# A feed-forward beside a recurrence: the gelus as one block on ACT, and fewer recurrence units planned around them

## Chip, core and metric

The kernel runs on one core of a Trainium2 chip, in one launch, in float32. The metric is the device time of one execution in microseconds. A core has five engines that matter here, each with its own in-order queue: PE (TensorE, matrix products and transposes), DVE (VectorE), ACT (ScalarE), POOL (GpSimd) and SP (SyncE, which issues most DMAs).

## What is computed

The input is 8 images of 384 channels and 32 x 32 pixels, so 8 sequences of 1024 tokens. Two layers follow each other. Cut to what matters here:

```python
# layer 0: RMS norm, then a selective recurrence in both directions
deltaA, deltaBu = exp(delta * A), (delta * u) * Bm
h[t] = deltaA[t] * h[t-1] + deltaBu[t]        # 16 states of 384 channels
y[t] = sum_n h[t, n] * Cm[t, n]
x = x + res_scale * ((fwd + bwd) * scale_mod + sigmoid(dwconv(xn)) * xn)
# layer 1
t = t + causal_attention(layernorm(t))         # 6 heads
# feed-forward, all of it per sequence; only the first 5 of 8 sequences are non-zero
y = layernorm(t) @ Wb1.T + b1                  # 384 -> 1536, weights binarized by group
hq = clip(y * 128 / (max(abs(y)) + 1e-5), -128 + 1e-5, 128 - 1e-5)
y2 = gelu(hq) @ Wb2.T + b2                     # 1536 -> 384
t = t + clip(y2 * 128 / (max(abs(y2)) + 1e-5), -128 + 1e-5, 128 - 1e-5)
```

The quantization divides by the maximum over the whole sequence. So no gelu may start before the last element of the first product is known, and no element of the output before the last of the second.

## The kernel before

The eight sequences are worked on in the order 0, 1, 2, 3, 5, 6, 4, 7. Each goes through three kinds of work: `before_scan` (norm, input projection L341, convolutions by taps L369 and L400, gates L434 and L453, the delta steps L518 to L531), the recurrence, and `attention` with `feed_forward` behind it for sequences 0 to 4.

**The recurrence** is cut into 768 units, 96 a sequence. A unit is two of the 16 states, one block of 128 channels and half of the tokens in one direction. `s_first` multiplies on POOL (L588) into one of six buffers g; `s_scan` makes two exponentials on ACT into two PSUM banks `da` (L601), two scans on DVE (L606), sometimes a copy of the carry on POOL (L611), and the second multiplication on POOL (L612); `s_sum` adds up eight 128 x 128 transposes on PE (L620), after which the g buffer is free. A slot of the plan issues the first multiplication of unit k + 2, the scan and second multiplication of unit k and the transposes of unit k - 1. POOL's order is pinned, so it is L588 of k + 2, then L612 of k. The loads of `bc`, `ud` and `dl` go through SP (line 112), as do those of the weights w1 and w2.

**The feed-forward** of a sequence is, in program order: layernorm; twelve blocks of 128 features in two halves, each three matmuls (L993), a bias-add on ACT (L1001), and per block a maximum on DVE (L1003); `quant_scale`, which reduces the maxima to one, spreads it with one transpose on PE (L960) and makes 128 / (max + 1e-5) in four small DVE operations (L962 to L965); four gelus on ACT of 128 x 3072 elements (L1018), each followed by the load of the table set that exponentials and logarithms use (L1019) and a clip on DVE (L1020); then for three blocks of 128 channels in two halves twelve matmuls each (L1038), a bias-add on ACT and a maximum on DVE; `quant_scale` again; and the output.

**The order of the work.** All of this is recorded as a list of steps with planned costs in us (`emit.of(...)`). The feed-forwards of sequences 0 to 3 are interleaved with the `before_scan` of sequences 5, 6, 4 and 7, by the share of the planned cost that each has used up (`spread_over`); the costs of both then count 0.6 (`JOINT`). The feed-forward of sequence 4 stands alone. The slots of the recurrence are spread evenly over the planned time of attention and feed-forward between due dates. So a step's planned cost decides how many slots, and how many steps of the other sequence, are issued around it; it costs nothing itself. A scheduler then moves instructions within priorities: `tc.high_priority(offset=60)` lifts a step's instructions ahead of others, `pin` (`tc.keep_in_program_order`) holds the order on their engine.

Of the kernel before, what the change touches and what calls it, by code (L numbers as in the profile page):

```python
# [11 lines left out]
AF = mybir.ActivationFunctionType  # L12
ALU = mybir.AluOpType
# [7 lines left out]
NC = C // P  # L21
# [9 lines left out]
NF = FF // P  # L31
GROUPS = 5
QMAX = 128.0
QEPS = 1e-5
QCLIP = QMAX - QEPS
# [11 lines left out]
LOG_EXP = "natural_log_exp_and_others"  # L47
# [7 lines left out]
def kernel(  # L55
# [16 lines left out]
    nc = tc.nc  # L72
    pin = tc.keep_in_program_order
# [13 lines left out]
    def btile(name):  # L87
        return big.tile([P, NC, L], F32, name=name, tag="big")

    def mtile(name, n=L):  # L90
        return mid.tile([P, n], F32, name=name, tag="mid")
# [7 lines left out]
    def bank(name, tag=None):  # L99
        if tag is None:  # L100
            turn[0] += 1
            tag = ("s", "pt")[turn[0] % 2]
        return ps.tile([P, HB], F32, name=name, tag=tag, bufs=BANKS[tag])

    def half(h):
        return slice(h * HB, (h + 1) * HB)

    def chunk(c):
        return slice(c * P, (c + 1) * P)

    def load(dst, src):
        nc.sync.dma_start(out=dst, in_=src)
# [167 lines left out]
    def layernorm(src, name, emit):  # L280

        dst = src
        st = {}
        for h in range(NH):

            @emit.of(6.0)
            def _(h=h):
                mean = mean_of(lambda c: src()[:, c, half(h)], f"mean_{name}_{h}")
                for c in range(NC):
                    nc.vector.tensor_tensor(  # L290
                        dst()[:, c, half(h)], src()[:, c, half(h)], mean, ALU.subtract
                    )
                st[h] = squares(dst(), h, name)

        for h in range(NH):

            @emit.of(6.0)
            def _(h=h):
                var = mean_of(lambda c: st[h][c], f"var_{name}_{h}")
                rstd_of(var, 1)  # L300
                for c in range(NC):
                    nc.vector.tensor_tensor(  # L302
                        dst()[:, c, half(h)], dst()[:, c, half(h)], var, ALU.mult
                    )
# [369 lines left out]
    def attention(b, emit_ffn, emit):  # L674
# [276 lines left out]
        if feeds:  # L951
            feed_forward(b, lambda: st["t2"], emit_ffn)


    def quant_scale(mx, name):

        col = small.tile([P, 1], F32, name=f"col_{name}", tag="col")
        nc.vector.tensor_reduce(col, mx, AX.X, ALU.max)
        row = bank(f"row_{name}", "s")
        nc.tensor.transpose(row[:, :P], col.to_broadcast([P, P]), ident)  # L960
        s = small.tile([P, 1], F32, name=f"qs_{name}", tag="qs")
        nc.vector.tensor_reduce(s, row[:, :P], AX.X, ALU.max)  # L962
        nc.vector.tensor_scalar(s, s, QEPS, None, ALU.add)
        nc.vector.reciprocal(s, s)
        nc.vector.tensor_scalar(s, s, QMAX, None, ALU.mult)  # L965
        return s

    def feed_forward(b, t, emit):
        st = {}

        @emit
        def _():
            st["xn"] = t()
            st["mxh"] = small.tile([P, NF], F32, name=f"mxh_{b}", tag="mxh", bufs=1)
            st["mxy"] = small.tile([P, NC], F32, name=f"mxy_{b}", tag="mxy", bufs=1)

        layernorm(t, f"nf_{b}", emit)
        for m in range(NF):
            for h in range(NH):

                @emit.of(3.1)
                def _(m=m, h=h):
                    if m % NC == 0 and h == 0:
                        st["h", m // NC] = btile(f"h{m // NC}_{b}")
                    if m % 2 == 0 and h == 0:
                        st["w1"] = mtile(f"w1_{b}_{m}").rearrange("p (c e) -> p c e", c=4)
                        load(
                            st["w1"][:, :NC, :],
                            w1s[:, m * P : (m + 2) * P].rearrange("(c p) e -> p c e", p=P),
                        )  # L990
                    hp = bank(f"hp_{b}_{m}_{h}", "s")
                    for c in range(NC):
                        nc.tensor.matmul(  # L993
                            out=hp,
                            lhsT=st["w1"][:, c, chunk(m % 2)],
                            rhs=st["xn"][:, c, half(h)],
                            start=(c == 0),
                            stop=(c == NC - 1),
                        )
                    hm = st["h", m // NC][:, m % NC, :]  # L1000
                    nc.scalar.activation(hm[:, half(h)], hp, AF.Identity, bias=b1t[:, m : m + 1])  # L1001
                    if h == NH - 1:
                        nc.vector.tensor_reduce(  # L1003
                            st["mxh"][:, m : m + 1], hm, AX.X, ALU.max, apply_absolute_value=True
                        )

        @emit.of(12.0)
        def _():
            st["s1"] = quant_scale(st["mxh"], f"h_{b}")


        for q in range(NF // NC):

            @emit.of(4.0)
            def _(q=q):
                hq = st["h", q]
                with tc.high_priority(offset=60):
                    nc.scalar.activation(hq, hq, AF.Gelu, scale=st["s1"])  # L1018
                    tc.keep_in_program_order(nc.scalar.preload_act_table_set(LOG_EXP))  # L1019
                nc.vector.tensor_scalar(hq, hq, QCLIP, None, ALU.min)  # L1020

        for m in range(NC):
            for h in range(NH):

                @emit.of(10.7)
                def _(m=m, h=h):
                    if m == 0 and h == 0:
                        st["y"] = btile(f"yf_{b}")
                    if h == 0:
                        for k in range(0, NF, 6):  # L1030
                            w = mtile(f"w2_{b}_{m}_{k}", 6 * P).rearrange("p (k e) -> p k e", k=6)
                            load(
                                w, w2s[k * P : (k + 6) * P, chunk(m)].rearrange("(k p) e -> p k e", p=P)
                            )
                            st["w2", k // 6] = w
                    yp = bank(f"yp_{b}_{m}_{h}", "s")
                    for k in range(NF):
                        nc.tensor.matmul(  # L1038
                            out=yp,
                            lhsT=st["w2", k // 6][:, k % 6, :],  # L1040
                            rhs=st["h", k // NC][:, k % NC, half(h)],
                            start=(k == 0),
                            stop=(k == NF - 1),
                        )
                    ym = st["y"][:, m, :]
                    nc.scalar.activation(
                        ym[:, half(h)], yp, AF.Identity, bias=vec[:, m, V_B2 : V_B2 + 1]
                    )
                    if h == NH - 1:
                        nc.vector.tensor_reduce(  # L1050
                            st["mxy"][:, m : m + 1], ym, AX.X, ALU.max, apply_absolute_value=True
                        )

        @emit.of(12.0)
        def _():
            st["s2"] = quant_scale(st["mxy"], f"y_{b}")

        for m in range(NC):

            @emit  # L1060
            def _(m=m):
                to = mtile(f"t3_{b}_{m}")
                load(to, spilled[b, "t2", m])
                for h in range(NH):
                    ym = bank(f"yq_{b}_{m}_{h}", "s")
                    nc.vector.tensor_scalar(
                        ym, st["y"][:, m, half(h)], st["s2"], QCLIP, ALU.mult, ALU.min
                    )
                    th = to[:, half(h)]
                    nc.vector.scalar_tensor_tensor(th, ym, -QCLIP, th, ALU.max, ALU.add)  # L1070
                nc.sync.dma_start(out=out[b, chunk(m), :], in_=to)
# [151 lines left out]
```

## Time and profile before

| | |
|---|---|
| median of 6 runs | 5051.09 us (5039.68 to 5060.6) |
| profiled execution, its own time | 5039.68 us |
| its span | 5037.9 us |
| granted PE clock, mean | 0.883 |
| gelus, L1018, 20 of 128 x 3072 | 2.856 us each |
| table loads at L1018 and at L1019 | 19 and 19, 1.283 us each |
| clips, L1020 | 1.753 to 3.874 us, median 1.761 |
| memory traffic | 138 GB/s over the span |

The profile is that of the fastest of the six runs; its span and its own time differ by 1.8 us. It begins with some 127 us in which POOL has no unit yet, and ends with some 205 us of the last attention, in which the recurrence is over. Between them lie four rounds of attention with a joint feed-forward (829 to 3543 us), two rounds of attention alone (3543 to 4270) and one of attention with the lone feed-forward (4270 to 4829).

How to read it: busy us of an engine are the union of its instructions. In a row of a group the number before the vertical bar is what the group works on, then follow its busy us and the mean ns of one, and behind the second bar the idle time of the engine just before its instructions, with what ended most of it. A matmul in float32 leaves two records. L620 records are one transpose each, eight a unit.

### The profile page before, as it was taken

What the parts mean: (1) busy time and instruction counts of PE and PEld (TensorE: products, weight loads), DVE (VectorE), ACT (ScalarE), POOL (GpSimd) and SP (SyncE); (2) the same over time, 40 slices, a digit from 0 to 9 for tenths busy, and PEclk for the clock granted to TensorE, in tenths of its full rate; (3) what the DMA queues carried; (4) which work ended last, traced back from release to release, by engine and by line L of the source; (5) the groups of instructions that cost most, each with busy time, mean ns of one, the idle gap of its engine ahead of it and who ended that gap; (6) DMA issues with size and microseconds to landing.
All of it is one profiled execution on the core that took longest, in us unless ns stands there. A gap on an engine that the chain in (4) does not pass through costs nothing. (4 is left out here: it accounts for less than half of the span.)

```text
span 5037.9 us, 50760 instructions
## 1 busy us (share of the span) xinstructions
PE 4092.0 (81%) x16458; PEld 2188.9 (43%) x16458; DVE 3599.8 (71%) x4780; ACT 2719.8 (54%) x4891; POOL 3691.0 (73%) x1944
## 2 busy tenths in 40 slices
PE   3687787878788888888797888888788978878899
PEld 1243343544434444444443445434444544444444
DVE  6887978677786778876678867678767666666523
ACT  4565664565645656545556446565365454464426
POOL 0578687987669986788876698768788978787710
PEclk7788797989889898888998899998998989989999
DMA  6554546324363334443334533335533324324210
GB/s 232 198 176 157 207 155 229 113 86 142 132 217 116 118 114 162 161 172 124 103 134 142 204 108 130 113 117 188 181 129 122 101 96 143 105 93 134 87 64 26
DMA packets 365010, 696.36 MB, mean 138 GB/s; under 512 B 30104, under 2 KB 88904, under 8 KB 364744
## 3 DMA queue, kind: packets, MB, share of 16 engines
q1 hardware_dynamic: 355232, 676.97, 39.6%
q10 hardware_dynamic: 9512, 16.15, 0.9%
q8 instruction: 130, 2.13, 0.2%
q14 instruction: 136, 1.11, 0.1%
HBM read 527.33 MB, written 165.68 MB: 138 GB/s over the span
## 5 line engine op out<-in xcount | busy, mean ns | idle before, releaser
L588 POOL TENSOR_TENSOR g<-ud,bc 128x1024 f32<-128x1024 f32 x768 | 1837.9, 2393 | 644.8 <-PE y L620 506.6
L612 POOL TENSOR_TENSOR g<-g,bc 128x1024 f32<-128x1024 f32 x768 | 1820.4, 2370 | 229.9 <-DVE g L606 177.3
L601 ACT ACTIVATE da<-dl,amat 128x512 f32<-128x512 f32 x1536 | 1056.4, 691 | 1486.6 <-DVE g L606 1443.9
L606 DVE TENSOR_TENSOR_SCAN g<-da,carry,g 128x512 f32<-128x512 f32 x768 | 958.3, 1272 | 408.4 <-POOL g L588 366.2
L606 DVE TENSOR_TENSOR_SCAN g<-da,g 128x512 f32<-128x512 f32 x768 | 906.8, 1211 | 472.7 <-POOL g L588 440.3
L620 PE MATMUL y<-ident,g 128*128 128x128 f32 x6144 | 935.0, 300 | 273.8 <-POOL g L612 214.2
L620 PEld LDWEIGHTS y<-ident,g 128*128 128x128 f32 x6144 | 774.1, 154 | 731.1 <-POOL g L612 340.5
L786 PE MATMUL s<-k,q 64*128 64x512 f32 (+3 forms) x1152 | 404.7, 609 | 126.0 <-DVE nm L800 114.9
L800 DVE CUSTOM_DVE_ANT_0 pr<-s,cmask 128x512 f32<-128x512 f32 (+3 forms) x576 | 301.0, 546 | 207.6 <-PE s L786 181.7
L810 ACT ACTIVATE pr<-pr,nm 128x512 f32<-128x512 f32 (+3 forms) x576 | 348.9, 607 | 139.6 <-DVE nm L800 137.8
L862 PE MATMUL pt<-ident,pr 128*128 128x128 f32 x1728 | 301.8, 305 | 72.3 <-ACT ptn L864 32.9
L993 PE MATMUL hp<-t,w 128*128 128x512 f32 x720 | 337.2, 613 | 26.7 <-DMA w<-w1s 13.8
L1038 PE MATMUL yp<-h,w 128*128 128x512 f32 x720 | 328.2, 613 | 9.8 <-DMA w<-w2s 9.8
L341 PE MATMUL in<-xn,win 128*128 128x512 f32 x576 | 296.1, 656 | 46.0 <-DVE xc L463 14.8
L862 PEld LDWEIGHTS pt<-ident,pr 128*128 128x128 f32 x1728 | 208.7, 153 | 234.0 <-ACT ptn L864 87.9
L875 PE MATMUL av<-ptn,v 128*64 128x512 f32 (+3 forms) x1152 | 273.3, 557 | 24.0 <-DVE o L889 16.2
L864 ACT COPY ptn<-pt 128x512 f32<-128x512 f32 (+3 forms) x576 | 255.1, 474 | 67.6 <-PE pt L862 66.2
L400 DVE SCALAR_TENSOR_TENSOR loc<-xn,vec,loc 128x496 f32<-128x496 f32 (+3 forms) x384 | 260.7, 723 | 23.6 <-ACT loc L389 22.2
L725 PE MATMUL qp<-t,wqk 128*128 128x512 f32 x576 | 261.2, 603 | 19.0 <-DVE t L302 13.5
L611 POOL COPY carry<-g 128x2 f32<-128x2 f32 x384 | 85.6, 223 | 242.8 <-DVE g L606 242.8
L786 PEld LDWEIGHTS s<-k,q 64*128 64x128 f32 x1152 | 139.2, 208 | 254.4 <-DVE nm L800 192.5
L1038 PEld LDWEIGHTS yp<-h,w 128*128 128x128 f32 x720 | 140.1, 199 | 177.3 <-issue 166.2
(155 smaller groups left out, 4803.0 us busy)
## 6 DMA issues: line engine op xcount, KB each, us to landing
bc<-rows SPq DMA_DIRECT2D x512, 512.0 KB, 4.0
dl<-sdl SPq DMA_DIRECT2D x160, 256.0 KB, 2.9
ud<-sud SPq DMA_DIRECT2D x160, 256.0 KB, 2.7
t<-st SPq DMA_DIRECT2D x63, 512.0 KB, 5.0
su<-u SPq DMA_DIRECT2D x48, 512.0 KB, 3.9
du<-su SPq DMA_DIRECT2D x96, 256.0 KB, 4.7
sdl<-du SPq DMA_DIRECT2D x96, 256.0 KB, 3.2
sud<-du SPq DMA_DIRECT2D x96, 256.0 KB, 2.5
```

What stands on the lines that cost most here:

```text
L341: nc.tensor.matmul(out=mp, lhsT=st["win", c][:, k, i, :], rhs=st["xn"][:, k, half(h)], start=(k == 0), stop=(k == NC - 1),)
L588: pin(nc.gpsimd.tensor_tensor(g, ud, sst["bc", 0, u.b, u.part, u.n], ALU.mult))
L601: nc.scalar.activation(da, sst["dl", u.b, u.c, u.part], AF.Exp, scale=amat[:, u.c, n : n + 1])
L606: nc.vector.tensor_tensor_scan(gi[:, ::step], da[:, ::step], gi[:, ::step], first, ALU.mult, ALU.add)
L612: pin(nc.gpsimd.tensor_tensor(g, g, sst["bc", 1, u.b, u.part, u.n], ALU.mult))
L620: nc.tensor.matmul(out=y[:, j, :], lhsT=g[:, i, chunk(j)], rhs=ident, is_transpose=True, start=(u.opens and i == 0 and j == 0), stop=(u.cl ...
L786: mm = nc.tensor.matmul(out=ss[e][:, : k1 - k0], lhsT=st["q"][rows_of(e), c, chunk(qi)], rhs=st["k"][rows_of(e), c, k0:k1], start=True, st ...
L800: nc.vector.tensor_tensor_reduce(out=x, in0=ss[e][:, :w], in1=mask, scale=-1.0, scalar=-MASKED, op0=ALU.add, op1=ALU.min, accum_out=m,)
L810: nc.scalar.activation(x, x, AF.Exp, bias=m, scale=-1.0, accum_out=rs[:, i, e, kb : kb + 1])
L862: nc.tensor.transpose(pt[:, chunk(i)], pr[:, e, chunk(j % QT)], ident)
L993: nc.tensor.matmul(out=hp, lhsT=st["w1"][:, c, chunk(m % 2)], rhs=st["xn"][:, c, half(h)], start=(c == 0), stop=(c == NC - 1),)
L1038: nc.tensor.matmul(out=yp, lhsT=st["w2", k // 6][:, k % 6, :], rhs=st["h", k // NC][:, k % NC, half(h)], start=(k == 0), stop=(k == NF - 1),)
```

## The change

Three things are changed in the feed-forward, and nothing else.

- The four gelus and the one table load behind them are one step and pinned to each other, with no load of the other set between them; the four clips follow, and are in the high-priority part too.
- The planned costs: of the two `quant_scale` steps 3 instead of 12 us each, and of all the gelus together 3 instead of 4 x 4. A feed-forward has 31 us less of planned cost, so fewer slots, and fewer steps of the other sequence's `before_scan`, are issued around these steps, and more elsewhere.
- `quant_scale` makes its scale with one DVE operation less: (max + 1e-5) / 128 in one, then the reciprocal.

```diff
         nc.vector.tensor_reduce(s, row[:, :P], AX.X, ALU.max)
-        nc.vector.tensor_scalar(s, s, QEPS, None, ALU.add)
+        nc.vector.tensor_scalar(s, s, QEPS, 1.0 / QMAX, ALU.add, ALU.mult)
         nc.vector.reciprocal(s, s)
-        nc.vector.tensor_scalar(s, s, QMAX, None, ALU.mult)
         return s
...
-        @emit.of(12.0)
+        @emit.of(3.0)
         def _():
             st["s1"] = quant_scale(st["mxh"], f"h_{b}")
 
 
-        for q in range(NF // NC):
-
-            @emit.of(4.0)
-            def _(q=q):
-                hq = st["h", q]
-                with tc.high_priority(offset=60):
-                    nc.scalar.activation(hq, hq, AF.Gelu, scale=st["s1"])
-                    tc.keep_in_program_order(nc.scalar.preload_act_table_set(LOG_EXP))
-                nc.vector.tensor_scalar(hq, hq, QCLIP, None, ALU.min)
+        @emit.of(3.0)
+        def _():
+            with tc.high_priority(offset=60):
+                for q in range(NF // NC):
+                    pin(nc.scalar.activation(st["h", q], st["h", q], AF.Gelu, scale=st["s1"]))
+                pin(nc.scalar.preload_act_table_set(LOG_EXP))
+                for q in range(NF // NC):
+                    nc.vector.tensor_scalar(st["h", q], st["h", q], QCLIP, None, ALU.min)
...
-        @emit.of(12.0)
+        @emit.of(3.0)
         def _():
             st["s2"] = quant_scale(st["mxy"], f"y_{b}")
```

The changed kernel is two lines shorter, so that its L1015, L1016 and L1018 are the gelus, the load and the clips, L992 the first product and L1036 the second.

## The prediction

> **What bounds the kernel now.** I read the page first, then the busy time stage by stage, then the waits of each engine inside the stages, then the timeline of the gelus, and last the order in which the two programs' instructions stand on each engine (an order has no times).
>
> The page, busy time of each engine:
>
> ```profile
> PE 4092.0 (81%) x16458; PEld 2188.9 (43%) x16458; DVE 3599.8 (71%) x4780; ACT 2719.8 (54%) x4891; POOL 3691.0 (73%) x1944
> ...
> L588 POOL TENSOR_TENSOR g<-ud,bc 128x1024 f32<-128x1024 f32 x768 | 1837.9, 2393 | 644.8 <-PE y L620 506.6
> L612 POOL TENSOR_TENSOR g<-g,bc 128x1024 f32<-128x1024 f32 x768 | 1820.4, 2370 | 229.9 <-DVE g L606 177.3
> ```
>
> No engine is full. POOL does 768 units of the recurrence, 3691/768 = 4.8 us each; its idle time before L588 is mostly a wait for PE's transposes (a free g buffer), so PE holds POOL back as often as the other way round. The average says little, so here is the second round by stage. Columns: us, then busy us (instructions) of PE, PEld, DVE, ACT, POOL, then PE's granted clock:
>
> ```profile
> 1494.00:1880.00 386.00, 325.83 (x1500) 181.09 (x1500) 275.36 (x399) 209.19 (x433) 335.45 (x173) 0.91 0.37 124
> 1880.00:1986.00 106.00, 98.99 (x350) 52.07 (x348) 88.47 (x107) 66.06 (x95) 70.87 (x38) 0.97 0.50 168
> 1986.00:2042.00 56.00, 34.18 (x101) 18.85 (x99) 41.82 (x44) 38.14 (x39) 41.26 (x24) 0.66 0.25 86
> 2042.00:2140.00 98.00, 87.58 (x270) 43.80 (x270) 81.86 (x83) 51.04 (x77) 76.71 (x40) 0.92 0.57 191
> 2140.00:2162.00 22.00, 15.39 (x53) 9.71 (x51) 21.16 (x29) 13.12 (x23) 13.16 (x6) 0.66 0.90 320
> ```
>
> These are attention with the layernorm after it, the first product (L993), the gap from its end to the second product, the second product (L1038) and the output. The first product is PE's (99 of 106 us) while POOL idles a third. In the gap nobody is full: PE 34, DVE 42, ACT 38, POOL 41 of 56 us. The four rounds with a joint feed-forward have gaps of 55, 56, 58 and 58 us, mean 57; the last feed-forward has 31. What the gap waits for, ACT first, then DVE, then POOL:
>
> ```profile
> 1998.35 1.28 ACT L1018 ACT_TABLE_LOAD   x1
> 1999.64 2.85 ACT L1018 ACTIVATE h<-h,qs_h 128x3072 f32<-128x3072 f32 x1
> 2002.51 1.28 ACT L1019 ACT_TABLE_LOAD   x1
> 2003.80 1.28 ACT L1018 ACT_TABLE_LOAD   x1
> ...
> 2018.88 1.28 ACT L1019 ACT_TABLE_LOAD   x1
> ```
>
> ```profile
> 2018.90 1.76 DVE L1020 TENSOR_SCALAR h<-h 128x3072 f32<-128x3072 f32 x1 [3.70 <-ACT h L1018]
> 2021.39 5.74 DVE L606 TENSOR_TENSOR_SCAN g<-da,g 128x512 f32<-128x512 f32 x5 [0.73 <-ACT da L601]
> ```
>
> ```profile
> 2022.67 0.18 POOL L611 COPY carry<-g 128x2 f32<-128x2 f32 x1 [9.97 <-DVE g L606]
> ```
>
> ACT is shut to the recurrence from 1998.35 to 2020.16, 21.8 us; DVE, in order, stands at the clips behind it; POOL idles 10 us. So the four gelus are in fact one block already, with eight switches in it. And PE, before it may start L1038, must transpose the units queued ahead: in the built order 10, 10, 10.75 and 11 of them in these gaps.
>
> **The change, part by part.**
>
> Table loads. The built order has 5 + 5 loads at the gelus instead of 19 + 19, and eight fewer elsewhere (seven at the L601 exponentials); 124 become 88. 36 x 1.283 us = 46 us of ACT, but ACT is 54% busy, so only what lies in a block counts: eight loads become two, 6 x 1.283 = 7.7 us per feed-forward, and the block is 2 x 1.283 + 4 x 2.856 = 14.0 us. The Trainium skill ("ScalarE: Activation LUTs", What ACT_TABLE_LOAD costs) puts a switch at 1283 ns plus a drain of about 1380 ns, 2.66 us. The row contradicts the second term: the load at 1998.35 ends at 1999.63 and the gelu starts at 1999.64; the next load starts 0.02 us after the gelu. By the rule the block would lose 16.0 us, 8.3 more per feed-forward and 33 over four; I use the row.
>
> The scale. One 0.13 us DVE operation goes from each of ten chains; in the trace L965 also stood one scan behind L964. At most 1.3 us each on the way to the gelus; I take 0, since the exponentials queued ahead of the gelus cover it, and keep 6 us over all.
>
> Less between maxima and second product. Units of the recurrence in each gap by PE's order: 10, 10, 10.75, 11, 9 become 6, 6, 4, 8, 8: 19 fewer. The four in_proj tiles of the other batch stay; four small xp products move into the first product. The new gap, for the second round, counted from the last transpose before the final L993 group:
> - POOL is six g buffers ahead there (at 1984.3 PE transposes unit 294 while POOL is past the first multiply of 298), so one more first multiply (2.4), one unit's scans (2.5), the last maximum (1.2), the row, and the scale: ready at about 8 us.
> - Gelus and clips: first operand at 8.3 + 1.28 + 2.86 + 1.76 = 14.2, the fourth at 22.8.
> - PE's own work until L1038: 2.6 (last L993 group) + 10.3 (24 records of 0.43) + 6 x 1.04 + 0.4 = 19.5.
> - SP: the w2 load now stands behind one more ud load, which waits until unit 307's first multiply has freed a buffer: about 21.5, and 4.5 to land (a bc load of like size takes 4.0): 26.
> The latest is the w2 load, 26; less the final group, a gap of 23. Lower bound 17 (PE's work alone), upper bound 6 x 4.8 + 13 (POOL idle while the block holds the scans, plus six ACT copies queued behind it) = 42, if POOL is not ahead.
> A rule of the skill speaks against the low end ("TensorE: Matmul & The Clock Gate", Part 1: after some 3.4 us idle the array runs at half clock). The row: eight transposes took 1.97 us in the gap (clock 0.66) against 1.04 in the first product (0.97). If the new gap still has idles, PE's 17 us become up to 31; if it runs dense, as the first product does, 17. I take 25 for the gap: 57 - 25 = 32 us, four times, 128. The last gap, 31 us with POOL busy 30.65, loses one unit: 5 us.
>
> What is moved. By PE's order the 19 units, and 3 from the stages behind, go to: layernorm plus first product, 109 become 122; attention, 423 become 432 (four of them in the last round). Their price is between PE's 1.04 us and POOL's 4.8.
> - Layernorm plus first product: POOL is idle 9 + 35 us per round, DVE is busy 28 + 88 of 145 us. 3.2 units bring 3.3 us of PE, 1.1 of xp products and some 8 us of scans. PE's price with a surcharge for DVE's order: 8 us per round, 32; 2 in the last.
> - Attention: PE 84%, POOL 87%, neither hides the other. The last attention beside the recurrence has 51.5 units and took 324 us (4270 to 4594), six others with 61 on average took 355: 31/9.5 = 3.3 us per unit. 9 x 3.3 = 29.
> - Second product: POOL enters it about 10 us behind, two more delta steps stand in it, and behind the clips on DVE now wait conv taps and then scans: +6 us per round, 24 (0 to 12 each). The output stage, where DVE is full (21.2 of 22), loses those two deltas, 2 x 4 x 0.7 = 5.6 us of DVE: -2 us per round, 8. Last round: two units fewer beside the product, -4.
>
> Sum: -128 - 5 - 4 + 32 + 2 + 29 + 24 - 8 = -58 us. I take -55, since part of the load's and the clip's chains is estimated. The profiled execution took 5039.7 (span 5037.9 and 1.8 around it), so 4985; it is the fastest of the six runs, and the median is 11 higher, so I forecast 5051 - 55 = 4996.
>
> **Rivals.**
> - B, the moved units pay POOL's price everywhere. The gap shrinks as above, but 22 units x 4.8 = 106 us come back, with 16 behind the gap and 8 for xp products and scans out of turn: -137 + 106 + 16 + 8 = -7, 5044. For it: POOL's 87% in attention. Against: its idle third in the first product.
> - C, slower: POOL is not ahead when the block begins. For it: POOL waited 11.8 us for a DVE scan just inside the second gap (1990.1), behind the other batch's taps, and the block then stops it again. Then the gap costs 42, saves 15 x 4 = 60, and the moved work costs 106 + 24 - 8: +62, 5113. It decides from a lead below three units at the last maximum.
> - D, larger gain: gap 17, PE's price everywhere (22 x 1.04 = 23) and nothing lost behind the gap: -160 - 9 + 23 + 8 = -138, 4913.
> - That the change doesn't do what it says is excluded for the table loads by the order (four gelus in a row, two loads). For the recurrence it is half true: six units remain, since PE's order lets the first product run behind them.
>
> **How the numbers follow.** The forecast has 0.50, B 0.17, C 0.28, D 0.05. The forecast's own range is 4945 (gap 17 and attention at 1.04 us per unit: 32 and 20 us less) to 5024 (gap 32: 28 more). Within 0.2% (10 us, about what a measurement of this kernel can tell from no change) lies most of B: 0.12; faster 0.55; slower C and the rest of B, 0.33. The range to hold it 8 in 10 leaves out D below and the worse half of C: 4935 to 5105.
>
> **What would show it.** In the changed profile: two table loads and four gelus per block, 14 us; gaps from the last L992 to the first L1036 of 20 to 28 us with PE over 70% busy; POOL idle 10 to 14 us once in each, behind the block; the first product 5 to 10 us longer, attention 0 to 5. Wrong would be: gaps over 36 us with POOL waiting for scans before the gelus start (C), or gaps short and attention longer by 10 us a round (B).

## The result, and the profile after

The changed kernel takes 5038.75 us (median of 23 runs) against 5047.97 us for the one before (46 runs): ratio 0.9982, interval 0.9977 to 0.9988, 9 us faster. A gain of 55 us was forecast.

The profiled execution of the changed kernel has a span of 5046.2 us, 8 longer than that of before: it is 9 us slower than the median of its kernel, and that of before is 8 us faster than its median. So stages are compared here for where time moved, and the medians for how much.

The page's engines and the two groups on POOL:

```profile
PE 4079.0 (81%) x16458; PEld 2182.4 (43%) x16458; DVE 3603.0 (71%) x4775; ACT 2666.7 (53%) x4850; POOL 3694.3 (73%) x1944
...
L588 POOL TENSOR_TENSOR g<-ud,bc 128x1024 f32<-128x1024 f32 x768 | 1839.2, 2395 | 656.9 <-PE y L620 500.5
L612 POOL TENSOR_TENSOR g<-g,bc 128x1024 f32<-128x1024 f32 x768 | 1821.7, 2372 | 183.0 <-DVE g L606 122.8
```

ACT is 53 us less busy; 46 were worked out for the loads. POOL's idle time has not changed: before 645 us at L588, 230 at L612 and 243 at the carry copy, after 657, 183 and 272; 1118 and 1112.

The second round by stage: attention, layernorm, first product, gap, second product, output.

```profile
1513.40:1866.10 352.70, 295.60 (x1386) 167.39 (x1386) 249.13 (x369) 188.01 (x398) 304.10 (x158) 0.89 0.37 126
1866.10:1906.40 40.30, 35.23 (x135) 19.03 (x133) 33.55 (x42) 25.24 (x43) 35.50 (x16) 1.00 0.31 101
1906.40:2026.80 120.40, 105.08 (x349) 53.68 (x350) 91.27 (x106) 63.65 (x93) 73.31 (x43) 0.91 0.46 160
2026.80:2069.30 42.50, 18.11 (x74) 10.41 (x72) 32.09 (x33) 30.89 (x33) 36.69 (x21) 0.73 0.20 59
2069.30:2171.10 101.80, 89.44 (x256) 43.45 (x257) 74.00 (x79) 48.21 (x73) 64.00 (x33) 0.88 0.53 174
2171.10:2197.20 26.10, 17.18 (x67) 10.56 (x65) 25.89 (x29) 15.07 (x26) 18.54 (x7) 0.73 0.69 245
```

The gap is down to 42.5 us, but PE is busy for only 18 of it, and the first product takes 120 us instead of 105. All four joint rounds together (us, cut at the first and last matmul of each stage, in one execution each):

```
              attention  layernorm  product 1   gap   product 2  output    sum
before          1412.0     158.4      413.5    235.0    365.1    129.7   2713.7
after           1432.8     190.1      446.6    164.9    401.7    103.9   2740.0
block_only      1415.2     158.8      414.4    212.6    372.2    119.6   2692.9
units_only      1456.4     163.4      416.9    166.5    374.0    125.5   2702.6
other_only      1418.2     176.2      437.5    159.6    415.7    102.6   2709.8
costs_only      1434.7     192.1      444.6    165.5    400.2    103.8   2740.9
```

(The last four are experiments below.) From before to after, the gaps give 70 us, the output stage 26; attention and layernorm take 53, the products 70. By this cut the gaps before are 58.8 us on average; the prediction's 57 begin 1.5 to 4 us after the last matmul. Outside these four rounds the changed kernel is shorter, 2306 us instead of 2324, and 12 of these 18 us lie in the last round, whose feed-forward stands alone (546.7 us instead of 559.1).

Where the new gap goes. The block on ACT, in the second round, is what the change says it is:

```profile
2042.38 1.28 ACT L1015 ACT_TABLE_LOAD   x1
2043.78 11.10 ACT L1015 ACTIVATE h<-h,qs_h 128x3072 f32<-128x3072 f32 x4
2054.90 1.28 ACT L1016 ACT_TABLE_LOAD   x1
```

From 2042.38 to 2056.18: 13.8 us, 14.0 were forecast, before it was 21.8. PE in the same gap:

```profile
2029.18 1.04 PE L620 MATMUL y<-ident,g 128*128 128x128 f32 x8
2042.58 0.45 PE L960 MATMUL row_h<-ident,col_h 128*128 128x128 f32 x1 [12.36 <-DVE col_h L958]
...
2056.36 1.09 PE L620 MATMUL y<-ident,g 128*128 128x128 f32 x8 [0.25 <-POOL g L612]
2069.22 1.19 PE L1036 MATMUL yp<-h,w 128*128 128x512 f32 x1 [11.77 <-DMA w<-w2s]
```

PE stands 12.4 us for the maximum and 11.8 us for w2. On DVE the last maximum stands behind the scans of six units that PE had not yet transposed when it began the last matmuls of the first product (2.5 units in the kernel before). The scans of three of them run after the end of the first product, at 2026.8, and wait for POOL's multiplications:

```profile
2033.94 2.34 DVE L606 TENSOR_TENSOR_SCAN g<-da,g 128x512 f32<-128x512 f32 x2 [1.93 <-POOL g L588]
2038.79 2.34 DVE L606 TENSOR_TENSOR_SCAN g<-da,g 128x512 f32<-128x512 f32 x2 [2.51 <-POOL g L588]
2041.04 1.19 DVE L1002 TENSOR_REDUCE mxh<-h 128x1 f32<-128x1024 f32 x1
```

POOL had fallen behind since a stretch inside the first product. DVE there, then POOL:

```profile
1990.50 4.52 DVE L400 SCALAR_TENSOR_TENSOR loc<-xn,vec,loc 128x465 f32<-128x465 f32 x7
...
1996.61 5.19 DVE L400 SCALAR_TENSOR_TENSOR loc<-xn,vec,loc 128x496 f32<-128x496 f32 x8
...
2006.43 1.22 DVE L606 TENSOR_TENSOR_SCAN g<-da,g 128x512 f32<-128x512 f32 x1
```

```profile
1993.08 2.36 POOL L588 TENSOR_TENSOR g<-ud,bc 128x1024 f32<-128x1024 f32 x1
2009.48 0.19 POOL L611 COPY carry<-g 128x2 f32<-128x2 f32 x1 [14.04 <-DVE g L606]
```

No scan runs between the taps from 1990 to 2006, though POOL had made the input of the next one by 1985.6. In the kernel before, such a stall ended inside the gap. POOL's waits for scans that ended in the second gap of before (us in total, times, longest):

```profile
POOL carry L611 <- DVE g L606: 21.8, 2, 11.8
```

and in the first product of after:

```profile
POOL g L612 <- DVE g L606: 14.5, 1, 14.5
POOL carry L611 <- DVE g L606: 14.0, 1, 14.0
```

Over the four joint rounds these waits, each counted in the stage where it ended, were 43 us in the first products, 99 in the gaps and 36 in the second products; now they are 118 (25 of them in a round where the profile names no releaser), 3 and 70: 178 and 191. The waits left the gaps, and about as much waiting appeared in the products.

### The profile page after: what moved, and what is told of

It is laid out like the page before. It is cut to its first block, busy times and chain, and to the rows that moved or that the text cites. A ratio compares the mean times of both kernels' runs of the same rounds, so it can differ in the third digit from the quotient of the medians.

```text
span 5046.2 us, 50731 instructions
## 1 busy us (share of the span) xinstructions
PE 4079.0 (81%) x16458; PEld 2182.4 (43%) x16458; DVE 3603.0 (71%) x4775; ACT 2666.7 (53%) x4850; POOL 3694.3 (73%) x1944
## 5 line engine op out<-in xcount | busy, mean ns | idle before, releaser
L588 POOL TENSOR_TENSOR g<-ud,bc 128x1024 f32<-128x1024 f32 x768 | 1839.2, 2395 | 656.9 <-PE y L620 500.5
L612 POOL TENSOR_TENSOR g<-g,bc 128x1024 f32<-128x1024 f32 x768 | 1821.7, 2372 | 183.0 <-DVE g L606 122.8
L620 PE MATMUL y<-ident,g 128*128 128x128 f32 x6144 | 922.6, 298 | 208.3 <-POOL g L612 130.0
L992 PE MATMUL hp<-t,w 128*128 128x512 f32 x720 | 339.6, 618 | 25.5 <-DMA w<-w1s 16.1
L1036 PE MATMUL yp<-h,w 128*128 128x512 f32 x720 | 331.8, 620 | 27.3 <-DMA w<-w2s 27.3
L341 PE MATMUL in<-xn,win 128*128 128x512 f32 x576 | 285.6, 641 | 33.3 <-DVE xc L463 12.5
L400 DVE SCALAR_TENSOR_TENSOR loc<-xn,vec,loc 128x496 f32<-128x496 f32 (+3 forms) x384 | 259.7, 723 | 20.3 <-ACT loc L389 19.0
L1036 PEld LDWEIGHTS yp<-h,w 128*128 128x128 f32 x720 | 142.0, 201 | 200.8 <-issue 177.8
```

The lines of the kernel that those rows point to most:

```text
L588: pin(nc.gpsimd.tensor_tensor(g, ud, sst["bc", 0, u.b, u.part, u.n], ALU.mult))
L612: pin(nc.gpsimd.tensor_tensor(g, g, sst["bc", 1, u.b, u.part, u.n], ALU.mult))
L620: nc.tensor.matmul(out=y[:, j, :], lhsT=g[:, i, chunk(j)], rhs=ident, is_transpose=True, start=(u.opens and i == 0 and j == 0), stop=(u.cl ...
L992: nc.tensor.matmul(out=hp, lhsT=st["w1"][:, c, chunk(m % 2)], rhs=st["xn"][:, c, half(h)], start=(c == 0), stop=(c == NC - 1),)
L1036: nc.tensor.matmul(out=yp, lhsT=st["w2", k // 6][:, k % 6, :], rhs=st["h", k // NC][:, k % NC, half(h)], start=(k == 0), stop=(k == NF - 1),)
```

## The experiments

Theory T: POOL's wait for scans behind the other sequence's DVE work only moves. Rival R: each moved unit pays POOL's price where it goes, whatever DVE does. All ratios are to the kernel before, run on the same chip.

**block_only** and **costs_only**: the two halves of the change.

block_only is the changed kernel with the planned costs of before:

```diff
-        @emit.of(3.0)
+        @emit.of(12.0)
         def _():
             st["s1"] = quant_scale(st["mxh"], f"h_{b}")
...
-        @emit.of(3.0)
+        @emit.of(16.0)
         def _():
             with tc.high_priority(offset=60):
...
-        @emit.of(3.0)
+        @emit.of(12.0)
         def _():
             st["s2"] = quant_scale(st["mxy"], f"y_{b}")
```

costs_only is the kernel before with `@emit.of(3.0)` for both scales and `@emit.of(0.75)` for each of the four gelus.

> The gelus as one block with two loads and the shorter scale, planned costs as before (12, 16, 12), so the same units in the gaps. If the block is what gained and the plan gave it back (both theories): the block is 7.7 us shorter in each of five feed-forwards and POOL's stall behind it with it, so 25 to 38 us faster than before. If ACT's block was hidden behind the taps of the other sequence on DVE: within 10 us of before.

> The small planned costs alone (3, 4 x 0.75, 3), gelus with their eight loads as before. Theory T (POOL's wait for scans behind the other sequence's taps on DVE only moves from the gap into the two products): 10 to 30 us slower than before, with gaps some 8 us longer than in the changed kernel. Rival R (each moved unit pays POOL's 4.8 us where it goes, which the shorter gap just pays back): within 10 us of before.

block_only: 5028.8 us, 0.9959 (0.9946 to 0.9971): 22 faster. costs_only: 1.0007 (0.9999 to 1.0016), no change. So the block gains, and the plan's small costs on top of it lose: 0.9982 - 0.9959 is 12 us, give or take 7. R said "within 10" for costs_only and T 10 to 30 slower; measured 4: R's side, not decided. T also said that the gaps of costs_only would be 8 us longer than those of the changed kernel. They are the same, 41.4 us against 41.2 on average, though 28 table loads stand at its gelus instead of 10: beside the small costs it is not the block that ends these gaps.

**before_no_taps**, **block_no_taps**, **after_no_taps**: the L400 taps are left out for the four joint sequences (the local convolution then has its centre tap only).

```diff
-                if k == 4:
+                if k == 4 or (diags is None and later is None):
                     continue
```

> The kernel before, without the eight depthwise taps of L400 for the four sequences that are prepared beside a feed-forward (48 DVE operations of 0.72 us a sequence, 35 us). Serves as the base for the next run. Both theories: faster than before by some 40 to 100 us, since DVE is full in the output stage and late in the first product.

> The changed kernel without the same taps. Theory T: with no taps ahead of the scans POOL keeps its lead of several units to the end of the first product, so the change is now worth what was forecast: 40 to 60 us less than before_no_taps, gaps of 20 to 28 us. Rival R: the taps don't matter to the change; within 15 us of before_no_taps, although the gaps shrink.

> The block with the planned costs of before, without the taps of L400 in the four joint sequences. With taps the block alone is 22 us faster, and the small costs on top take 13 us back. If the taps are what takes them back, the changed kernel without taps (0.9860 of before) lies 15 us or more below this one; if not, within 8 us of it.

0.9912 (0.9898 to 0.9925), 0.9880 (0.9863 to 0.9897) and 0.9860 (0.9847 to 0.9874): the block takes 16 us off, the small costs 10 more, give or take 11. With the taps the small costs add 12. So the taps account for some 22 us (give or take 13) of what was lost, but even without them the whole change is worth 26, below T's 40.

**after_w2early** and **after_split_w2**: the first w2 loads are issued at the ninth block of the first product, in the second together with the cut below.

```diff
+                    if m == 8 and h == 0:
+                        for k in range(0, NF, 6):
+                            w = mtile(f"w2_{b}_0_{k}", 6 * P).rearrange("p (k e) -> p k e", k=6)
+                            load(w, w2s[k * P : (k + 6) * P, chunk(0)].rearrange("(k p) e -> p k e", p=P))
+                            st["w2", k // 6] = w
...
-                        for k in range(0, NF, 6):
+                        for k in range(0, NF, 6) if m > 0 else ():
```

> The changed kernel with the first two w2 loads issued beside the ninth block of the first product instead of at the second product, so SP no longer holds them behind ud and bc loads. PE waited 27.3 us for w2 in the changed kernel's trace. If that wait sets the gap's end: 15 to 27 us faster than the changed kernel. Theory T (POOL and DVE set the pace, PE's wait is covered by them later): within 8 us of the changed kernel.

> The changed kernel with the cut gate steps and the early w2 load, both moves of the plan kept. If the waits that came with the other sequence's steps (PE for w2, 9.8 to 27.3 us; POOL for scans behind taps) are what separates the changed kernel from units_only: 40 to 55 us faster than before. If what it is is the work itself, moved into the products: 25 to 38, as after_split alone.

0.9967 (0.9954 to 0.9980) and 0.9935 (0.9922 to 0.9949). The first closes the gaps from 41 to 28 us on average, near the 25 forecast, and the second to 20. Yet the first is only 8 us faster than the changed kernel, and the second no faster than after_split (0.9937), whose gaps are 34: the second products grow from 402 to 431, and from 380 to 429. Closing the gap further by itself brings little.

**after_split**, **block_split**, **before_split**, **units_split** and **block_split_w2**: the other sequence's gate step of 14 us is cut into three. (Not shown: the gate step of 10 us in the preparation of the first sequence is cut likewise.)

```diff
-                accs = [local(c, h) for h in range(NH)]
+                accs = st["accs"]
...
-                emit(gates, 14.0)
+                for h in range(NH):
+                    emit(lambda h=h, taps=taps: taps(h), 5.0)
+                emit(gates, 4.0)
```

> The changed kernel with each gate step of the other sequence cut into three (taps of one half, taps of the other, the rest), planned at 5, 5 and 4 us instead of 14 at once, so scans can stand between the taps on DVE. Theory T: POOL's waits for scans of 12 to 27 us shrink, 15 to 50 us faster than the changed kernel. Rival R (each moved unit pays POOL's price): no difference over 10 us.

> The block of gelus with the planned costs of before, and the gate steps of the other sequence cut into three as in after_split. The block alone took 22 us off, the cut took 21 us off the changed kernel. If both hold side by side: 35 to 45 us faster than before. If the cut only mends what the small planned costs did: 20 to 25.

> The kernel before, with the other sequence's gate steps cut into three. If cutting the taps apart helps wherever they stand: some 20 us faster than before, as on the block (22) and on the changed kernel (21). If it helps only beside the block: within 8 us.

> units_only with the gate steps of the other sequence cut into three. The units' move took 30 us off the block, the cut 22 off the block and 21 off the changed kernel. If both are separate waits: 65 to 80 us faster than before, 4970 to 4985. If the cut mends the same waits as leaving the other sequence's steps in the gap does: 45 to 55 faster, as units_only.

> As block_split, with the first w2 loads issued beside the ninth block of the first product as well. In the changed kernel that took 5 us off while it closed the gaps from 41 to 28 us; here the gaps do not wait for w2, so within 8 us of block_split.

The cut takes 23 us off the changed kernel (0.9937, 0.9925 to 0.9949) and 23 off the block (0.9913, 0.9901 to 0.9926), but 7 off the kernel before (0.9987, 0.9979 to 0.9995) and nothing off units_only (0.9905, 0.9891 to 0.9918). block_split_w2 is 0.9923 (0.9910 to 0.9936), as block_split. So taps in one piece do cost; but the cut helps the block as much, where the plan was left alone, so it is not simply a repair of what the small costs did. These totals are net of something else: the cut also reaches the sequences prepared ahead of the first round. In the traces the joint rounds become 17 to 38 us shorter with it in all four pairs, and the stretch ahead of them 8 to 15 us longer.

**after_pinmax** and **before_pin**: exponentials, scans and the last maxima are held in program order.

```diff
-            nc.vector.tensor_tensor_scan(
+            pin(nc.vector.tensor_tensor_scan(
                 gi[:, ::step], da[:, ::step], gi[:, ::step], first, ALU.mult, ALU.add
-            )
+            ))
...
+                    held = pin if m >= 10 else lambda i: i
```

The exponentials get the same `pin`, and `held` goes around the bias-adds and maxima of the first product, where it pins those of the last two blocks.

> The changed kernel with exponentials, scans, the last two blocks' bias-adds and maxima held in program order, so the last maximum stands 5 units earlier on DVE (after the scan of unit 299 instead of 304 in the second round) and 3 instead of 6 units of transposes stand in the gap. If the late maximum (PE waited 41 us for it at L960) makes the gap: 30 to 45 us faster than the changed kernel. Theory T: the moved wait comes back in the products, 0 to 15 us faster. The held order moves transposes elsewhere too, which the next run is the base for.

> The kernel before with the same order held. Base for after_pinmax: the difference of the two is what the change is worth when the plan is followed. If the plan's few units in the gap are worth what was forecast: after_pinmax 40 to 60 us below this one. Theory T: 0 to 20 us, beside the 22 us of the block alone.

1.0654 (1.0640 to 1.0667) and 1.0753 (1.0739 to 1.0767). The held order costs 380 us by itself; on that base the change is worth 53 us (give or take 10), with gaps of 22 instead of 65 us. The forecast's size comes out where the late maximum is gone, but in a kernel that is otherwise much slower, so this is a hint and not a proof.

**before_pool_light** and **after_pool_light**: the second multiplication for one of a unit's two states only (the other state is not multiplied by C).

```diff
-        pin(nc.gpsimd.tensor_tensor(g, g, sst["bc", 1, u.b, u.part, u.n], ALU.mult))
+        pin(nc.gpsimd.tensor_tensor(g[:, 0, :], g[:, 0, :], sst["bc", 1, u.b, u.part, u.n][:, 0, :], ALU.mult))
```

> The kernel before, with the recurrence's second multiplication on POOL (L612) done for one of a unit's two states only, so a unit costs POOL some 3.6 us instead of 4.8. Base for the next run. If POOL's 4.8 us a unit hold attention and the rest back: 150 to 400 us faster. If PE and DVE do: under 100.

> The changed kernel with the same half of the second multiplication left out; the same units are moved as in the full one. Theory R (the change's gain was eaten by POOL's price of the units moved into attention and layernorm): with a unit a quarter cheaper and POOL idle more, the change is worth 35 to 60 us against before_pool_light. Theory T (the scans stand behind the other sequence's work on DVE, whatever POOL costs): 0 to 20 us.

0.9266 (0.9248 to 0.9284) and 0.9252 (0.9238 to 0.9266): 371 us for a cheaper unit, so POOL matters much; but the change is worth 7 us there too (give or take 12), not R's 35 to 60. POOL's price alone is not what ate the gain. R falls in that form.

**units_only** and **other_only**: the plan's effect taken apart, beside the block. The small costs go either to the slots of the recurrence alone, or to the spreading of the other sequence's steps alone.

```diff
         @emit.of(12.0)
+        @slots_see(3.0)
         def _():
             st["s1"] = quant_scale(st["mxh"], f"h_{b}")
...
-            fed = [(f, JOINT * us) for f, us in fed]
+            fed = [(f, JOINT * getattr(f, "us", us)) for f, us in fed]
+        elif fed:
+            fed = [(f, getattr(f, "us", us)) for f, us in fed]
```

`slots_see` hangs a second cost on a step, by which it counts for the slots; this is units_only, and other_only has the two costs the other way round.

> The block, and the small planned costs for the placing of the recurrence alone; the steps of the other sequence are spread by the old costs, so its taps, xp products and deltas stand in the stages where they stood. By PE's order 10 of the 18 units leave the gaps. If moving units is what gave the gain back: 5 to 15 us slower than the block alone (5029). If the other sequence's steps did it: 5 to 30 us faster than the block alone, since 10 units fewer stand in the gaps.

> The block, and the small planned costs for the spreading of the other sequence's steps alone; the recurrence's slots go by the old costs (10 units still leave the gaps, because the scheduler ends the first product later). If the other sequence's work on DVE, moved out of the gap into the two products, gave the gain back: 8 to 25 us slower than the block alone. If the units did: within 5 us of it.

units_only: 4993.6 us, 0.9900 (0.9885 to 0.9915), 50 us faster than before and 30 (give or take 10) faster than the block. other_only: 0.9964 (0.9950 to 0.9977), as the block. So the block and the units' move are together worth nearly what was forecast (55), as long as the other sequence's steps stay in the gap. Of the kernels that leave no work out, units_only is the fastest, ahead of both kernels. Moving those steps as well costs 41 us (0.9900 to 0.9982, give or take 8).

That units_only comes near 55 is in part luck, since it gets there by another road. Its gaps are 41.6 us and not 25, and its joint rounds are no shorter than those of block_only in the traces (2703 us against 2693): the gaps give 46 us and attention takes 41. What is clearly shorter is the last round, where no other sequence stands beside: 543.4 us against 559.0. All six kernels with the old slots there (held order and left-out work aside) take 558.8 to 559.3 us, all seven with the new ones 541.1 to 548.1. The rest of the 30 us its trace, 14 us slower than the median, does not show.

What PE waits for differs between the two moves. Before:

```profile
PE yp L1038 <- DMA w<-w2s: 9.8, 4, 4.6
...
PE row_h L960 <- DVE col_h L958: 1.5, 2, 1.3
```

after:

```profile
PE row_h L960 <- DVE col_h L958: 43.6, 5, 12.8
...
PE yp L1036 <- DMA w<-w2s: 27.3, 4, 11.8
```

units_only:

```profile
PE yp L1044 <- DMA w<-w2s: 13.9, 5, 4.4
...
PE row_h L960 <- DVE col_h L958: 3.8, 3, 2.3
```

other_only:

```profile
PE yp L1044 <- DMA w<-w2s: 36.1, 6, 14.8
...
PE row_h L960 <- DVE col_h L958: 33.7, 5, 10.1
```

The waits for the maximum and for w2 come with the other sequence's steps, not with the units. These waits alone do not explain the 41 us: other_only has 70 us of them too and is no slower than the block. The table of stages says more. Moving the steps lengthens layernorm and the products by 84 us either way: from 945 us in block_only to 1029 in other_only, and from 954 in units_only to 1038 after. In other_only the gaps give 53 us for it. Beside the moved units they give 2, since they are 41.6 us on average with the units moved, 39.9 with the steps moved and 41.2 with both: the second move buys nothing more in the gap. Attention and output give back 45 us in the changed kernel, so that 37 remain in the traces, near the 41 of the medians.

## Why the forecast was wrong, step by step

Term by term, for the changed kernel, by the cuts of the stage table (us; one execution each, as above):

```
                               forecast   traces
gaps, joint rounds                 -128      -70
layernorm and first product         +32      +65
attention, joint rounds             +10      +21
second product                      +24      +37
output                               -8      -26
two rounds of attention alone        +6       -6
last round                           +6      -12
```

- **The block**: right. 13.8 us of 14.0; worth 22 us by itself, where 7.7 us in each of four gaps would be 31. In the last round it gave nothing (559.0 us in block_only, 559.1 before). The row against the drain held: the first gelu starts 0.1 us or less after the load.
- **The gap of 25 us**: wrong, 41 measured. The step that failed is "POOL is six g buffers ahead there", and with it "ready at about 8 us". When the first product's last matmuls begin, POOL had finished 5 more first multiplications than PE had transposed units in each round of the kernel before; in the joint rounds of the changed kernel the lead is 3, 2, 3 and 2. Where the other sequence's steps stay (units_only) it is 6, 5, 5 and 5, and without the taps (after_no_taps) it is back at 6, 4, 5 and 5, so the taps ahead of the scans take it away (with it back the gaps are 33 us, still not 25). In the second round the block began 15.6 us after the first product's end, in the others 21, since the last maximum ended 7.7 to 15.5 us after it (3.7 to 5.2 before). In the lone feed-forward the lead is still 5, the maximum ended 4.0 us after, and the gap fell from 32.5 to 24.8 us, near the 26 forecast for it. PE's own work was right: 18.1 us in the second gap (granted clock 0.73), 17 in the sum. C named the lost lead, and its 42 us are the measured gap, but in part by luck: they hold 13 us of POOL's idling behind the block, and in the new gaps POOL waited for scans for 3 us in all.
- **What moves beside the units**: a term that was mis-sized, and with 41 of the missing 46 us the dearest. "The four in_proj tiles of the other batch stay; four small xp products move" is right by count, but was read from PE's order alone and priced at 1.1 us a round, within a term of 8 that covered the units too. On DVE more moves: the first product and the gap held 127 of the conv taps L369 and now hold 85, layernorm and the second product 17 and now 59; the second product has 95 DVE operations of the delta steps instead of 59. (The taps L400 stay, 126 and now 113 of 192 in the first product.) Of these the sum had only the second product's, at 24 us. The price is some 10 us a round.
- **Units in attention and layernorm**: mis-sized, and no single price fits. 14.6 units more in the four joint rounds came with 53 us, beside steps that moved with them; four more in the last attention came with 3.7 us, where 13 were taken.
- **The w2 load**: named as the last to arrive, and it was, in three of four gaps; but with the load moved ahead the time hardly follows.
- **Rival B** gave 7 us, near the measured 9, but by the wrong road: its short gap did not come, and with a unit 1.2 us cheaper on POOL its 22 units would have cost 26 us less (an estimate from these numbers), while the change still gives 7.
- **The range** holds the measured 5038.75 us, near B's 5044 and not near its likeliest part. What else a planned cost moves was not asked.

Of theory T, the first half stands: the waits moved, relief of POOL (7 us) or of the w2 load (8 us) did not bring the gain back. The second half, that the taps are the reason, stands only in part, since without them the change was worth 26 us and not 40, and it gave no account of units_only and of after_pinmax. Open remains how the 41 us divide. The taps L400 may be some 22 of it by the kernels without them, if the units' own gain is the same there, which no run shows; the cut gives the same 23, but to the block as well. What the conv taps L369, the deltas and the copies on ACT take is not taken apart. units_only, units_split and block_split all end near 0.990 to 0.991, but the traces speak against a common limit: the joint rounds take 2703, 2682 and 2660 us there, the rest 2303, 2323 and 2345. A kernel with the joint rounds of block_split and the small costs for the last feed-forward alone was not run.

## What to carry to other kernels

A planned cost is a lever on everything that is spread by it, so ask for each list that uses it what moves, on every engine, and change the cost for one list at a time: here that is 50 us against 9. The length of a gap on one engine is no measure of the gain: three kernels with gaps of 41 us were 0, 9 and 50 us faster than before (costs_only, the changed kernel, units_only), one with 20 us was 33 and one with 52 us 44. Where a wait is taken out, look for it in the stages beside it: 178 us of waiting for scans became 191 in other places. And cut the whole span, not only the stages that were changed on purpose: the gain that the traces show most clearly here lies in the last round.

## What the chip showed that was not expected

The clips became slower: median 1.76 us before, 3.51 in block_only. Slow ones are found only with an instruction on POOL beside them; that they follow each other closely is not enough: in the traces of before, block_only and after, the 17 clips with no POOL instruction beside them take 1.75 or 1.76 us, six of them right behind another one, and of the other 43 many take up to 3.92. In block_only, DVE and then POOL:

```profile
2008.83 5.19 DVE L1018 TENSOR_SCALAR h<-h 128x3072 f32<-128x3072 f32 x2 [0.31 <-ACT h L1015]
```

```profile
2006.86 3.86 POOL L588 TENSOR_TENSOR g<-ud,bc 128x1024 f32<-128x1024 f32 x1
2010.67 1.72 POOL L611 COPY carry<-g 128x2 f32<-128x2 f32 x1
2012.47 3.74 POOL L612 TENSOR_TENSOR g<-g,bc 128x1024 f32<-128x1024 f32 x1
```

Both sides pay: POOL's multiplications take 3.7 to 3.9 us instead of 2.4, its small copy 1.72 instead of 0.2, beside a clip. The Trainium skill ("SBUF — State Buffer", Who interferes with whom) says that DVE in a mode that uses two ports, which a tensor_scalar can enter, and POOL lock each other out, each for a whole instruction. The durations here agree in kind: the first of these clips has 1.9 us of POOL's multiplication still to run beside it and takes 3.5 us instead of 1.76. Which mode the clips ran in no trace shows, and no run isolates it.
